# A gated recurrent layer on one core: the order of work before the first step

## The chip, the cores and the metric

The kernel runs on one core of a Trainium2 chip. The metric is the device time of one execution in microseconds (us). The kernel before took 1697.89 us, the median of three runs (1697.15 to 1697.95).

## What is computed

The input x holds 8 sequences of 512 time steps with 512 features. A recurrent layer with a state of 512 values for each sequence runs over the steps and its states are added to x:

```python
def step(h, x_t):
    fused = sigmoid(concatenate([x_t, h], axis=-1) @ w_W + w_b)
    hidden_state, output_state = split(fused, 2, axis=-1)
    memory_state = x_t @ wx_W + wx_b + hidden_state * (h @ wh_W + wh_b)
    h_new = output_state * h + (1.0 - output_state) * tanh(memory_state)
    return (h_new, h_new)
_, hs = scan(step, h0, swapaxes(x, 0, 1))
return x + swapaxes(hs, 0, 1)
```

All numbers are float32. A step needs the state of the step before it, so the 512 steps follow each other; the products of x don't need the state and can be made ahead.

## The kernel before

The state lies transposed: units on the 128 partitions, in four blocks `k` = 0 to 3 of 128 units, the 8 sequences in the free dimension. Blocks 0 and 1 are half A, blocks 2 and 3 half B, with tiles of their own (`hTA`, `hTB`). Four steps make a group (`GS = 4`, so 32 columns of state or of x: 4 steps x 8 sequences), and 16 steps make a chunk of x (`TC = 16`, tiles `xin`, 32 chunks).

A matrix product has a 128x32 block of the state or of x as its stationary operand and a block of weights as the moving one. Its result is 32 rows high, so four products, for `j` = 0 to 3, are put side by side on the four column groups of TensorE and write to the four quarters of the partitions of one PSUM bank. All products go through the helper `mm` (L149). Products accumulate in PSUM, and only one with `start=True` begins anew.

There are eight PSUM banks. Six of 128 columns, `R`, `G` and `H`, in two sets that alternate by group (`banks`), hold the sums from which a step's gates are read. Two of 512 columns (`xps`) hold what x and the biases give for a group: `prefill` (L188) is a generator that makes, for one block `k` at a time, the four products of x with 384 columns of `wx` and yields. `spread` (L200) copies a third of such a bank to `R`, `G` or `H` on ScalarE, `turn_x` (L205) transposes the remaining part into `md1` on VectorE, and `seed` (L184) writes the biases, kept in the tile `bias`, back to the bank with a ScalarE copy, so that it can take the group after next.

Order is that of the program, engine by engine, from `tc.manual_schedule()` (L142) on. Ahead of that line a scheduler may move instructions; the loads and memsets lie there. SyncE (SP) issues all large loads in one queue: x chunk 0 (L87, called at L97), four transfers of `wx` (L101, one for each `k`), six of `wh` (L106: one for each of `k` = 0, 1, 2 and three, R, G and H, for `k` = 3), then the chunks 1 to 3 of x, which the steps 0 to 2 ask for. The state `hin` (L96) and the four bias rows (`rows4`, L94, one partition of each quarter) are asked for on ScalarE's queue.

What PE does before the steps: each of the six banks is zeroed by four products of a zeros tile (L155), both `xps` banks get the biases by products of `ones` and `rows4` with `start=True` (L158), a copy of the second is kept in `bias` (L162), and the two groups' x products follow, alternating by `k` (L218). Then come 16 products of zeros into a bank that doesn't mind them (`warm`, L169, four in each call, called four times at L222). `spread`, `turn_x` and `seed` for group 0 follow.

Step 0 has an order of its own, `FIRST` (L28), in which each "-" is a call of `warm`; `R0` is the four products of bank R with block 0 of the state. Each `k` needs its own transfer of `wh`. All other steps use `ORDER` (L26). Behind the products of each step one piece of `prefill` for the group after next is taken (L249), in step 0 that is block 0 of group 2, which is steps 8 to 11.

The rest of a step: VectorE transposes R, ScalarE makes the sigmoid, and so on over `turn_h`, `turn_z`, `memory` and `update` to the new state, half A before half B. GpSimd adds the state to x (L351) for the output tile `ot`, which SP stores for each chunk.

## Time and profile before

| | us |
|---|---|
| median of 3 runs | 1697.89 |
| the profiled execution | 1697.85 |
| its span, from first to last instruction | 1696.1 |
| PE busy (share) | 1683.8 (99%) |
| VectorE, ScalarE, GpSimd busy | 1087.7, 922.8, 230.1 |
| first product of PE | 1.59 |
| x products done, zero products of L222 begin | 16.82 |
| first product with the state (step 0) | 17.69 |
| first product of step 1, of step 2 | 24.32, 27.69 |
| last product ends, last store is issued | about 1692, 1693.69 |

The span is counted from the first instruction, and all times below are us from there. "PE" in a profile is the matmul side of TensorE, "PEld" its loading of weights. All matmuls stand under L150, the body of `mm`, so they are told apart by their tiles: `R<-zeros` is a zeroing product, `xp<-rows,ones` a bias product, `xp<-wx,xin` an x product and `R<-wh,hTA` one with the state. A float32 matmul appears as two records, so four products are "x8".

### The profile page before, as it was taken

The numbers are of one execution on the slowest core, as the hardware profiler recorded it, in microseconds if no ns is written. First come the engines' busy times: TensorE is split into PE (matmuls) and PEld (weight loads), VectorE is DVE, ScalarE is ACT, GpSimd is POOL, SyncE is SP. The second block draws the span as 40 slices with busy tenths as digits, with TensorE's granted clock in tenths as the row PEclk, the third lists the DMA queues.
The fourth block names the chain that finished last, engine by engine and source line by source line (L and its number), as shares of the span: only waits on it lengthen the run. The fifth ranks groups of instructions, "written<-read, shape, count | busy, mean of one in ns | idle before, by whom it ended". The sixth has DMA issues, their size and how long they took to land.

```text
span 1696.1 us, 121805 instructions
## 1 busy us (share of the span) xinstructions
PE 1683.8 (99%) x53440; PEld 1467.6 (87%) x53440; DVE 1087.7 (64%) x8229; ACT 922.8 (54%) x5121; POOL 230.1 (14%) x1031
## 2 busy tenths in 40 slices
PE   8999999999999999999999999999999999999998
PEld 6888888888888888888888888888888888888887
DVE  4666666666666666666666666666666666666666
ACT  3555555555555555555555555555555555555554
POOL 0111111111111111111111111111111111111111
PEclk9999999999999999999999999999999999999999
DMA  4000000000000000000000000000000000000000
GB/s 177 17 4 17 17 17 17 17 5 17 17 17 17 5 17 17 17 17 5 17 18 17 17 15 6 17 17 17 17 4 17 17 17 17 5 17 11 11 11 10
DMA packets 11485, 30.88 MB, mean 18 GB/s; under 512 B 1348, under 2 KB 1604, under 8 KB 10952
## 3 DMA queue, kind: packets, MB, share of 16 engines
q1 hardware_dynamic: 10800, 23.07, 4.0%
q8 instruction: 417, 6.83, 1.6%
q14 instruction: 116, 0.95, 0.2%
q10 hardware_dynamic: 152, 0.02, 0.0%
HBM read 14.70 MB, written 8.39 MB: 14 GB/s over the span
## 4 chain that ended last, share of the span: by engine, by line
PE 99%; DVE 1%; DMA 0%; ACT 0%; issue 0%; ACTq 0%; DVEq 0%
PE R L150 26%; PE G L150 26%; PE H L150 26%; PE xp L150 20%; DMA rows<-in_bias_dram 0%; DVE md1A L290 0%; DVE hTA L256 0%; ACT hd0A L178 0%; ACT hTA L178 0%; DVE tz L272 0%; DVE bias L162 0%; ACTq L94 0%; DVE rows L92 0%; DVE tr L272 0%; ACT hTB L178 0%
## 5 line engine op out<-in xcount | busy, mean ns | idle before, releaser
L150 PEld LDWEIGHTS R<-wh,hTA 128*32 128x32 f32 x8192 | 243.3, 135 | 212.2 <-DVE hTA L256 212.2
L150 PE MATMUL xp<-wx,xin 128*32 128x384 f32 x4096 | 426.7, 486 | 0.2 <-DVE bias L162 0.2
L272 DVE STREAM_TRANSPOSE tr<-R 128x64 f32<-128x64 f32 x1024 | 194.9, 229 | 313.4 <-PE R L150 313.4
L351 POOL TENSOR_TENSOR ot<-xin,hTB 128x16 f32<-128x16 f32 x511 | 127.6, 250 | 1458.6 <-DVE hTB L256 1366.8
L150 PE MATMUL R<-wh,hTA 128*32 128x128 f32 x8192 | 321.4, 273 | 2.8 <-DVE hTA L256 2.8
L150 PE MATMUL H<-wh,hTB 128*32 128x128 f32 x8192 | 321.3, 273 | 0.0
L150 PE MATMUL R<-wh,hTB 128*32 128x128 f32 x8192 | 321.1, 273 | 0.0
L150 PE MATMUL G<-wh,hTB 128*32 128x128 f32 x8192 | 321.0, 273 | 0.0
L150 PE MATMUL H<-wh,hTA 128*32 128x128 f32 x8192 | 321.0, 273 | 0.0
L150 PE MATMUL G<-wh,hTA 128*32 128x128 f32 x8192 | 321.0, 273 | 0.0
L178 ACT ACTIVATE hd0B<-tz 128x16 f32<-128x16 f32 x512 | 114.8, 224 | 304.9 <-DVE tz L272 304.9
L178 ACT ACTIVATE md0A<-tr 128x16 f32<-128x16 f32 x512 | 120.6, 236 | 256.8 <-DVE tr L272 256.8
L150 PEld LDWEIGHTS G<-wh,hTA 128*32 128x32 f32 x8192 | 250.2, 136 | 0.0
L150 PEld LDWEIGHTS H<-wh,hTA 128*32 128x32 f32 x8192 | 249.8, 136 | 0.0
L150 PEld LDWEIGHTS H<-wh,hTB 128*32 128x32 f32 x8192 | 244.1, 122 | 0.1
L150 PEld LDWEIGHTS G<-wh,hTB 128*32 128x32 f32 x8192 | 243.9, 122 | 0.0
L150 PEld LDWEIGHTS R<-wh,hTB 128*32 128x32 f32 x8192 | 241.2, 122 | 0.1
L256 DVE TENSOR_TENSOR_SCAN hTA<-hd0A,hTA 128x48 f32<-128x48 f32 x512 | 132.0, 258 | 149.2 <-ACT hTA L178 149.2
L256 DVE TENSOR_TENSOR_SCAN hTB<-hd0B,hTB 128x24 f32<-128x24 f32 x1024 | 157.8, 196 | 103.8 <-ACT hTB L178 103.8
L178 ACT ACTIVATE hd0A<-tz 128x16 f32<-128x16 f32 x512 | 118.6, 232 | 111.2 <-DVE tz L272 111.2
L290 DVE STREAM_TRANSPOSE md1A<-G 128x64 f32<-128x64 f32 x512 | 158.9, 310 | 28.7
L178 ACT ACTIVATE hTB<-hTB 128x16 f32<-128x16 f32 x512 | 122.0, 238 | 81.9 <-DVE hTB L256 81.2
(50 smaller groups left out, 1661.9 us busy)
## 6 DMA issues: line engine op xcount, KB each, us to landing
xin<-in_x_dram SPq DMA_DIRECT2D x32, 256.0 KB, 4.0
out_dram<-ot SPq DMA_DIRECT2D x31, 256.0 KB, 2.5
wx<-in_wx_dram SPq DMA_DIRECT2D x4, 768.0 KB, 6.4
wh<-in_wh_dram SPq DMA_DIRECT2D x3, 768.0 KB, 9.6
wh<-in_wh_dram SPq DMA_DIRECT2D x3, 256.0 KB, 12.2
out_dram<-ot SPq DMA_DIRECT2D x1, 192.0 KB
rows<-in_bias_dram ACTq DMA_DIRECT2D x4, 2.0 KB
out_dram<-ot SPq DMA_DIRECT2D x1, 64.0 KB, 1.5
```

The source lines that it names most:

```text
L150: nc.tensor.matmul(out_, lhsT, rhs, start=start, stop=False, skip_group_check=True)
L178: inst = nc.scalar.activation(out_, in_, func, **kw).ins
L256: nc.vector.tensor_tensor_scan(*[t_[:, :, c_].rearrange("p n c s -> p (n c s)") for t_ in (out_, d0, d1)], 0.0, ALU.mult, ALU.add,)
L272: inst = nc.vector.transpose(t_.rearrange("p c n -> p (c n)"), raw[n][hf]).ins
L290: nc.vector.transpose(md1[hf][g % 2][:, :, :, 0].rearrange("p n c -> p c n"), raw["h"][hf])
L351: return engine.tensor_tensor(ot[:, t, 2 * hf : 2 * hf + 2, :].rearrange("p c n -> p n c"), xins[c][:, 2 * hf : 2 * hf + 2, t * B : t * B ...
```

## The change

The two `xps` banks are zeroed by zero products as the six others are, for which the tile of zeros grows to 512 columns. Their biases come by products without `start=True` behind the x products: that of bank 0 behind `k` = 1, that of bank 1 behind `k` = 2. The four calls of `warm` in front of step 0 are gone. `seed(0)` is gone: in step 0, ahead of `R1`, four bias products with `start=True` fill bank 0 again, and `bias` is copied from there by VectorE. `FIRST` has six "-" in place of twelve. The tile of an x chunk has its two halves of 8 steps one after the other, `[P, 2, 4, 64]`, so that chunk 0 can be fetched in two transfers: the first half in front, the second behind all of `wh`; all readers of x use `x_of`. The host lays x out to match. The request for `hin` stands ahead of the bias rows. The first activation, which loads a table, is a sigmoid in place of a tanh.

```diff
-FIRST = "R0 G0 H0 - - - - R1 G1 H1 - - - - R2 G2 H2 - - - - R3 G3 H3"
+FIRST = "R0 G0 H0 - - R1 G1 H1 - - - - R2 G2 H2 R3 G3 H3"
...
-    def load_x(c):
+    def load_x(c, half=slice(0, 2)):
+
         if c < NCH:
-            t_ = xin_p.tile([P, NQ, TC * B], F32, tag="xin", name=f"xin_{c}")
-            nc.sync.dma_start(out=t_, in_=x[c].rearrange("p (k n) -> p k n", k=NQ))
-            xins[c] = t_
+            if c not in xins:
+                xins[c] = xin_p.tile([P, 2, NQ, TC * B // 2], F32, tag="xin", name=f"xin_{c}")
+            nc.sync.dma_start(
+                out=xins[c][:, half], in_=x[c].rearrange("p (e k n) -> p e k n", e=2, k=NQ)[:, half]
+            )
+
+    def x_of(c, k, t, n):
+
+        e, t = divmod(t, TC // 2)
+        return xins[c][:, e, k, t * B : (t + n) * B]
+
+    hin = const.tile([P, NQ, B], F32, name="hin")
+    nc.scalar.dma_start(out=hin, in_=h0)
...
-    hin = const.tile([P, NQ, B], F32, name="hin")
-    nc.scalar.dma_start(out=hin, in_=h0)
-    load_x(0)
+    load_x(0, 0)
...
+    load_x(0, 1)
...
-    zeros = const.tile([P, 128], F32, name="zeros")
+    zeros = const.tile([P, 512], F32, name="zeros")
...
-    nc.scalar.activation(const.tile([P, 1], F32, name="table"), zeros[:, :1], AF.Tanh)
+    nc.scalar.activation(const.tile([P, 1], F32, name="table"), zeros[:, :1], AF.Sigmoid)
...
-    for t_ in list(banks[0].values()) + list(banks[1].values()):
+    for t_ in list(banks[0].values()) + list(banks[1].values()) + xps:
         for j in range(NQ):
-            mm(t_[32 * j : 32 * j + 32, :], zeros[:, :32], zeros, start=True)
-    for t_ in xps:
-        for j in range(NQ):
-            mm(t_[32 * j : 32 * j + 32, :], ones[:, j], rows4, start=True)
-    bias = const.tile([P, 512], F32, name="bias")
-    nc.vector.tensor_copy(bias, xps[1])
+            mm(t_[32 * j : 32 * j + 32, :], zeros[:, :32], zeros[:, : t_.shape[1]], start=True)
...
+    def bias_of(q, start=False):
+
+        for j in range(NQ):
+            mm(xps[q][32 * j : 32 * j + 32, :], ones[:, j], rows4, start)
+
     def warm():
         for j in range(NQ):
-            mm(banks[1]["H"][32 * j : 32 * j + 32, :], zeros[:, :32], zeros)
+            mm(banks[1]["H"][32 * j : 32 * j + 32, :], zeros[:, :32], zeros[:, :128])
...
     for k in range(NQ):
         for it in both:
             take(it, 1)
-    for _ in range(4):
-        warm()
+        if k > 0 and k < 3:
+            bias_of(k - 1)
     spread(0, "RGH")
     for e in range(NQ):
         turn_x(0, e)
-    seed(0)
+    bias = const.tile([P, 512], F32, name="bias")
...
+            if n == "R1" and i == 0:
+                bias_of(0, start=True)
+                nc.vector.tensor_copy(bias, xps[0])
```

In `prefill` and in the adds of GpSimd the slices of `xins[c]` are replaced by `x_of(...)` with the same elements.

More of the change, by code (lines that the diff above doesn't have):

```diff
@@ L194, in prefill @@
                     xps[g % 2][32 * j : 32 * j + 32, 64:448],
-                    xins[c][:, k, t0 * B : t0 * B + 32],
+                    x_of(c, k, t0, GS),
                     wx[:, k, j, :],
@@ L328, in tile_cond_rnn_residual @@
                 ot[:, t, :2, :].rearrange("p c n -> p n c"),
-                xins[c][:, :2, t * B : t * B + B].rearrange("p c n -> p n c"),
+                x_of(c, slice(0, 2), t, 1).rearrange("p c n -> p n c"),
                 state(0, T),
@@ L352, in add @@
                 ot[:, t, 2 * hf : 2 * hf + 2, :].rearrange("p c n -> p n c"),
-                xins[c][:, 2 * hf : 2 * hf + 2, t * B : t * B + B].rearrange("p c n -> p n c"),
+                x_of(c, slice(2 * hf, 2 * hf + 2), t, 1).rearrange("p c n -> p n c"),
                 state(hf, i + 1),
@@ L420 @@
     xd = units(_np.moveaxis(x, 2, 0))
-    xd = xd.reshape(128, 4, Bn, NCH, TC).transpose(3, 0, 1, 4, 2)
+    xd = xd.reshape(128, 4, Bn, NCH, 2, TC // 2).transpose(3, 0, 4, 1, 5, 2)
     xd = c_(xd).reshape(NCH, 128, 4 * TC * Bn)
```

## The prediction

> **What bounds the kernel now.** I read the page first: TensorE (PE) is busy for 99% of the span, its granted clock is near full, and VectorE, ScalarE and the DMA engines have room. Then the chain of waits, in order of time:

> ```profile
> 2.50 5.42 DMA rows<-in_bias_dram
> 7.92 0.14 issue
> 8.05 3.46 PE xp L150 x16
> ...
> 11.53 0.70 DVE bias L162
> 12.23 0.04 issue
> 12.28 4.72 PE xp L150 x56
> ...
> 24.01 0.27 DVE hTA L256
> 24.28 0.04 issue
> 24.32 0.32 PE R L150
> ```

> See that the start hangs on the bias rows (landed at 7.92), on 16 records of bias products, on x products, and at 24.32 on the first new state, where step 1 begins. From there PE works without a break. Between 24.32 and 1690 the waits of PE alone add up to this:

> ```profile
> PE R L150 <- DVE hTA L256: 2.8, 8, 0.4
> ```

> So 511 steps take about (1692 - 24.32)/511 = 3.26 us each, PE-bound, and what the change can move is the instant at which step 1 starts. The timeline of PE up to there:

> ```profile
> 8.05 3.41 PE L150 MATMUL xp<-rows,ones 128*32 128x512 f32 x16 [3.67 <-DMA rows<-in_bias_dram]
> 11.28 0.83 PE L150 MATMUL xp<-wx,xin 128*32 128x384 f32 x8
> 12.28 4.72 PE L150 MATMUL xp<-wx,xin 128*32 128x384 f32 x56 [0.17 <-DVE bias L162]
> 16.82 1.06 PE L150 MATMUL H<-zeros 128*32 128x128 f32 x32
> 17.69 0.40 PE L150 MATMUL R<-wh,hTA 128*32 128x128 f32 x8
> ...
> 22.49 0.40 PE L150 MATMUL G<-wh,hTB 128*32 128x128 f32 x8
> 22.71 0.59 PE L150 MATMUL H<-wh,hTB 128*32 128x128 f32 x7
> ```

> One matmul is two records, and four matmuls on the four column groups (a "quad" below) run side by side. Prices of a quad from start to start: 128 columns 0.43 us cold (R at 1.59, G at 2.02) and 0.22 warm (17.69, 17.91); 384 columns 0.65 warm (seven quads, 12.28 to 16.82); 512 columns 1.7 cold (two in 3.41), and by columns 0.65 x 512/384 = 0.86 warm. That cold and warm exist is seen in the windows (last columns: granted clock, DMA share, GB/s):

> ```profile
> 4.28:7.69 3.41, 0.10 (x4) 0.00 (x0) 2.15 (x11) 0.02 (x1) 0.00 (x0) 1.00 1.01 391
> 7.69:11.10 3.41, 3.05 (x16) 0.90 (x20) 0.00 (x0) 0.00 (x0) 0.00 (x0) 0.50 1.03 429
> 11.10:14.50 3.40, 3.23 (x40) 1.07 (x36) 1.01 (x5) 0.00 (x0) 0.00 (x0) 1.00 1.01 403
> 14.50:17.90 3.40, 3.40 (x72) 1.99 (x68) 0.51 (x4) 0.84 (x4) 0.00 (x0) 1.00 1.01 404
> 17.90:21.30 3.40, 3.40 (x134) 3.40 (x129) 0.00 (x0) 1.62 (x2) 0.00 (x0) 1.00 0.82 314
> ```

> PE idle for one stretch of 3.41 us, then half clock for the next. (Before 4.28 the records hold no clock; the 0.43 quads show that it was cold.) And the DMA share is 1.0 until about 20: the loads of weights are the second limit, now hidden. From the DMA section of each issue (KB, us from issue to landing):

> ```profile
> wh<-in_wh_dram SPq DMA_DIRECT2D x2, 256.0 KB, 12.2
> xin<-in_x_dram SPq DMA_DIRECT2D x1, 256.0 KB, 11.2
> ```

> The last wh transfer, issued at 8.43, lands at 20.6; the next x chunk, issued at 10.02, at 21.2. The trace's completion records give the others: wx 6.05, 8.17, 10.01, 11.86; wh 13.74, 15.70, then 18.71, 19.34, 19.97, 20.61. The jump of 3.0 us before 18.71 is one engine: the other fifteen finish that transfer by 17.55. At 15.94 a 16 KB instruction transfer of 0.97 us sits on the same DMA engines (the DMA view from 15.9 on shows it as queue q8), and the laggard stays about 1.1 us behind to the end.

> [...] the trace has 3% (fell) and 79% (2.69 of 3.41 from 0.87, rose). [...]

> **The change part by part.** Origin as in the profile before. Less x in front: the first transfer shrinks from 256 to 128 KB; the queue moves about 0.41 MB per us, so all of wx and wh land 0.3 us sooner. From landing to PE I take 0.13 (7.92 to 8.05).

> *In front.* The zeros tile is four times as wide: its memset costs 485 ns (rows, 128x512) instead of 165, so PE starts at 1.59 + 0.32 = 1.91. Six 128-wide quads, 6 x 0.43, to 4.47; then two 512-wide, warm 1.72 or cold 3.4, to 6.2 or 7.9. No wait for the bias rows. The h0 request was already ahead of the rows on ScalarE's queue in the trace (0.74), so that edit is worth 0.

> *x products.* Chunk 0 (two quads, 1.3): 6.2 to 7.5, wx landed at 5.75. Chunk 1: wx at 7.87, 8.0 to 9.3. Bias of bank 0, 0.86 warm instead of 1.7 cold, to 10.2 (rows in at 7.9). Chunk 2 to 11.5, bias of bank 1 to 12.3, chunk 3 to 13.6. Before: 16.82. That is 3.2 us won, and the 16 zero products behind it (four quads, 0.87) go too. The copies to R, G, H follow bank 0 by 0.25 to 0.84 us (16.42 to 17.01 before) and lie beside bank 1's last quad.

> *Step 0.* It had 12 zero quads; 6 remain, and the new bias quad (0.86) equals 4: net 0.43 less. R0 G0 H0 0.65 to 14.3, two zero quads to 14.7, the bias quad (waits for VectorE's four transposes, done by about 14.4) to 15.6. Its copy to SBUF, 0.69 on VectorE, has nothing behind it before the R transposes; ScalarE loses the copy of 0.59 and the second table load of 1.28, both of which lay in its idle time: 0. wh of k = 1 at 15.4: 15.6 to 16.2; four zero quads to 17.1. If the instruction transfer, which now comes earlier since PE consumes sooner, slows an engine there, up to 1.2 later; this is still hidden, for now the loads bind: k = 2 at 18.71 - 0.3 + 0.13 = 18.5, done 19.2; R3 19.2; G3 at 19.97 - 0.17 = 19.8; H3 at 20.44 to 20.66.

> *The end of step 0.* Before, step 1 started 24.32 - 22.49 = 1.83 after G3, over transposes, sigmoid, scan, tanh and update. So the state is there at 19.8 + 1.83 = 21.6. The x product of group 2 now reads the second half of x, queued behind all wh on SP. SP issues it once the third wx has landed (9.7)[...]; half of the 0.62 between the last wh and x1 gives 20.6, PE at 20.75, done at 21.4. Also its wait for the bias copy (done by about 16.5) is void. The x chunks 1 to 3 are asked for one issue later (0.33 each); nobody reads them before group 4. On GpSimd's first add the added wait (x half) is met long before.

> Step 1 starts at max(21.4, 21.6) = 21.6 instead of 24.32: 2.7 us. H3's half of the state is behind A's update on VectorE in both, so nothing is lost there. The remaining steps have the same instructions; the x layout only changes strides (GpSimd adds, 250 ns two times a step, idle else). The profiled execution took 1697.85 us for a span of 1696.1; 1697.85 - 2.7 = 1695.15. The median of before, 1697.89, lies 0.04 above it, so I forecast 1695.1.

> **Unknown costs.** Clock at the start: if the rise at 4.28 is missed, the x side ends at about 14.8 to 15.2 instead of 13.6; R3 would be ready at about 17.7 + 1.6 and the wh wait of 19.2 covers it, so 0 to 0.1. The collision with the instruction transfer: from 0 (everything after lands 1.1 sooner) to a second one on the same engine (another 1.1 later). A clock drop in step 0: 0 to 1.7 per half-clock window of dense work.

> **The rivals.**
> *B, no laggard.* The transfer of instructions falls earlier and costs the last wh nothing. G3's weights then land at 18.85 - 0.3, G3 runs at 18.7, step 1 starts at 20.5: 3.8 us, 1694.0. For it: only one engine of sixteen lagged, and why it lost 1.1 to 1.5 us to a 0.97 us transfer is not shown. Against: the queue is full, so a lag once caught has no time to vanish.
> *C, the second half of x comes late.* A second instruction transfer (20.63 before, about 18.5 now) hits the lagging engine[...]: x at 21.7, x product done at 22.5 and the step likewise 0.9 to 1.4 later: 1696.3. Against: before, successive ones did not show on one engine.
> *D, the clock falls in step 0.* The zero products before R3 are gone and PE waits for wh: from 17.0 to 20.4 it may be busy for only 1.1 of 3.41 us, 32%. If that counts as idle, the next window of dense work runs at half clock: 1.7 lost, 1696.8.
> *E, slower than before.* The same drop, but PE does not recover in one window: each dense half-clock window costs 1.71 us, so from 2.7/1.71 = 1.6 windows on the change loses. Two give 1695.1 + 3.4 = 1698.5; slower by over 0.2% needs 3.6 windows. Against: from 21.6 on PE is fully busy, and before, one such window (7.69 to 11.10) was enough.

> **How the numbers follow.** Forecast 42% (own range 1694.4 to 1695.8), B 37%, C 8%, D 9%, E 4%. B is high because the lag rests on one instance. The range 1693.6 to 1696.9 takes in B, C and D. 0.2% (3.4 us) is about what a measurement of this kernel can tell from no change; the bound is 1694.5. Faster by more: nine tenths of B (34) and a quarter of the forecast's cases (11), 45%. Slower by more than 3.4 us: 2%. The rest, 53%, within.

> **What would show it.** Right: the zero quads end by 6 to 8; the last x product before 15.3; PE idle only in step 0, ended by DMA of wh; R<-wh,hTA of step 1 at about 21.6; later steps unchanged. B: that start at about 20.5. C: PE waiting for xin at the end of step 0. D, E: granted clock 0.5 after 18. Wrong altogether if steps behind step 1 differ by more than 5 ns each (2.7/511).

## The result and the profile after

| | before | after |
|---|---|---|
| median of 22 runs, us | 1698.36 (1697.15 to 1698.88) | 1695.11 (1694.78 to 1695.78) |
| profiled execution | 1697.85 | 1695.25 |
| its span | 1696.1 | 1693.5 |
| x products done | 16.82 | 14.33 (13.03 + 2 x 0.65) |
| first product of step 1 | 24.32 | 21.46 |

The ratio is 0.9982, with a 95% interval from 0.9976 to 0.9989: 3.25 us less by the medians, 2.6 by the two profiled executions. The three runs of before that the prediction knew had 1697.89 as their median, the 22 have 1698.36; that is half a microsecond of the difference.

The timeline of PE in the changed kernel, from the zeroing of the x banks on (start, duration, what, and in brackets the idle time ahead of it and what ended it):

```profile
4.55 3.07 PE L159 MATMUL xp<-zeros 128*32 128x512 f32 x16
7.45 2.75 PE L159 MATMUL xp<-wx,xin 128*32 128x384 f32 x32
10.03 1.03 PE L159 MATMUL xp<-rows,ones 128*32 128x512 f32 x8
...
13.03 1.46 PE L159 MATMUL xp<-wx,xin 128*32 128x384 f32 x16
14.73 0.45 PE L159 MATMUL R<-wh,hTA 128*32 128x128 f32 x8 [0.24 <-DMA wh<-in_wh_dram]
...
19.72 0.44 PE L159 MATMUL G<-wh,hTB 128*32 128x128 f32 x8 [0.30 <-DMA wh<-in_wh_dram]
20.36 0.44 PE L159 MATMUL H<-wh,hTB 128*32 128x128 f32 x8 [0.20 <-DMA wh<-in_wh_dram]
20.77 0.85 PE L159 MATMUL xp<-wx,xin 128*32 128x384 f32 x8
21.46 0.67 PE L159 MATMUL R<-wh,hTA 128*32 128x128 f32 x16
```

Three new waits, all ended by a transfer of wh, none of which was there before. The bias rows end no wait any more: their products stand at 10.03, where the rows have long landed, and a quad (four products side by side) of 512 columns takes 0.86 there (10.03 to 10.88), not 1.7. The chain of waits says the same in another way:

```profile
1.64 6.15 DMA wx<-in_wx_dram
7.79 0.02 issue
7.81 0.33 SPq L114
8.14 0.04 issue
8.18 12.13 DMA wh<-in_wh_dram
20.32 0.04 issue
20.36 0.44 PE H L159 x8
20.80 0.83 PE xp L159 x8
```

Up to 20.32 the path is loads, where before it was bias rows, x products and zero products. It is followed by the last wh (H of k = 3), the x product and step 1. The windows, to be held against those before (busy time of PE, PEld, VectorE, ScalarE, GpSimd, then granted clock, DMA share and GB/s):

```profile
4.28:7.69 3.41, 3.41 (x32) 1.07 (x28) 2.81 (x17) 0.02 (x1) 0.00 (x0) 1.00 1.01 413
7.69:11.10 3.41, 3.41 (x44) 1.20 (x40) 0.00 (x0) 0.00 (x0) 0.00 (x0) 1.00 1.02 427
```

PE is busy throughout where it stood idle (4.28 to 7.69), and the window after it has the full clock instead of half. The 1.00 of the first of these windows holds from 6.91 on alone: the clock record begins there, and up to then the zero products of 512 columns went at about the half clock's pace (2.90 for two quads, 4.55 to 7.45, where two of 0.86 would be 1.72). The steps themselves are as they were: measured at the update of half A, a step takes 3.264 us before and 3.265 after in the median, and from the first to the last update it is 1668.15 before and 1668.24 after.

### The profile page after: what moved, and what is told of

Its sections match the earlier page's. It is cut to its first block, busy times and chain, and to the rows that moved or that the text cites. A ratio compares the mean times of both kernels' runs of the same rounds, so it can differ in the third digit from the quotient of the medians.

```text
span 1693.5 us, 121691 instructions
## 1 busy us (share of the span) xinstructions
PE 1684.1 (99%) x53384; PEld 1466.7 (87%) x53384; DVE 1088.0 (64%) x8229; ACT 921.2 (54%) x5119; POOL 229.2 (14%) x1031
## 4 chain that ended last, share of the span: by engine, by line
PE 98%; DMA 1%; DVE 0%; ACT 0%; issue 0%; SPq 0%
PE R L159 26%; PE G L159 26%; PE H L159 26%; PE xp L159 19%; DMA wh<-in_wh_dram 1%; DMA wx<-in_wx_dram 0%; DVE md1A L302 0%; DVE hTA L268 0%; ACT hd0A L187 0%; ACT hTA L187 0%; DVE tz L284 0%; SPq L109 0%; SPq L89 0%; SPq L114 0%; ACT hTB L187 0%
## 5 line engine op out<-in xcount | busy, mean ns | idle before, releaser
L159 PE MATMUL xp<-wx,xin 128*32 128x384 f32 x4096 | 433.7, 486 | 0.0
L159 PE MATMUL R<-wh,hTA 128*32 128x128 f32 x8192 | 328.6, 273 | 2.8 <-DVE hTA L268 2.5
L159 PE MATMUL G<-wh,hTB 128*32 128x128 f32 x8192 | 328.1, 273 | 0.3 <-DMA wh<-in_wh_dram 0.3
L159 PE MATMUL H<-wh,hTB 128*32 128x128 f32 x8192 | 328.0, 273 | 0.2 <-DMA wh<-in_wh_dram 0.2
L159 PE MATMUL R<-wh,hTB 128*32 128x128 f32 x8192 | 328.1, 273 | 0.0
L159 PE MATMUL G<-wh,hTA 128*32 128x128 f32 x8192 | 328.1, 273 | 0.0
L159 PE MATMUL H<-wh,hTA 128*32 128x128 f32 x8192 | 328.1, 273 | 0.0
L159 PEld LDWEIGHTS H<-wh,hTA 128*32 128x32 f32 x8192 | 259.4, 137 | 0.0
L159 PEld LDWEIGHTS G<-wh,hTA 128*32 128x32 f32 x8192 | 259.3, 137 | 0.0
L159 PEld LDWEIGHTS G<-wh,hTB 128*32 128x32 f32 x8192 | 250.4, 122 | 0.6 <-DMA wh<-in_wh_dram 0.6
## 6 DMA issues: line engine op xcount, KB each, us to landing
xin<-in_x_dram SPq DMA_DIRECT2D x31, 256.0 KB, 3.2
out_dram<-ot SPq DMA_DIRECT2D x31, 256.0 KB, 2.4
wh<-in_wh_dram SPq DMA_DIRECT2D x3, 256.0 KB, 11.9
```

What stands on the lines that cost most here:

```text
L159: nc.tensor.matmul(out_, lhsT, rhs, start=start, stop=False, skip_group_check=True)
```

## The experiments

Twelve runs follow, each measured beside the kernel before on the same chip. Since that neighbour moved between 1697.76 and 1698.36 from one set of runs to the next, each is given with its own.

| run | edit | median | its before | step 1 starts (profile) |
|---|---|---|---|---|
| e1 | before, fewer zero products | 1695.58 | 1698.02 | 22.35 |
| e2 | after, all zero products back | 1697.26 | 1698.02 | 23.80 |
| e3 | after, x chunk 0 in one transfer | 1695.16 | 1698.02 | 21.41 |
| e4 | after, no zero product in step 0 | 1695.00 | 1698.02 | 21.32 |
| e5 | before, PE kept busy until the rows land | 1696.73 | 1697.76 | 22.40 |
| e6 | after, banks zeroed by 128-row products | 1695.31 | 1697.76 | 21.44 |
| e7 | after, x products in the waits | 1695.11 | 1697.76 | 21.59 |
| e8 | after again | 1694.92 | 1697.83 | 20.98 |
| e9 | e2, quads as 128-row products | 1697.68 | 1697.83 | 23.35 |
| e10 | before, quads as 128-row products | 1699.56 | 1697.83 | 26.55 |
| e11 | e7, other order | 1695.58 | 1697.83 | 21.30 |
| e12 | e2, four quads as one of 512 columns | 1696.18 | 1698.25 | 23.08 |

**e1: the zero products alone.**

```diff
-FIRST = "R0 G0 H0 - - - - R1 G1 H1 - - - - R2 G2 H2 - - - - R3 G3 H3"
+FIRST = "R0 G0 H0 - - R1 G1 H1 - - - - R2 G2 H2 R3 G3 H3"
...
-    for _ in range(4):
-        warm()
```

> The kernel before with one part of the change alone: the four warm calls in front of step 0 are gone and FIRST is the new one (six zero quads instead of twelve). Theory (loads of wh bind as soon as PE's own order is shorter): x side ends at 16.8 as before, R3 at about 20.1, G3 at 20.3, H3 just behind the last wh (20.7), step 1 starts at about 22.2 instead of 24.3; about 2.2 us less than before (1696.2 of 1698.4). Rival 1 (the zero products are needed for the clock): half clock after 18, gain under 0.5 us or a loss. Rival 2 (PE's time simply adds up and no load binds): ten quads of 0.22, R3 waits for nothing, PE shows no DMA wait.

Measured: 2.44 less than its neighbour, ratio 0.9985 (0.9979 to 0.9992), and step 1 at 22.35. The waits of PE from 4 to 26 us (time waited for, number, longest):

```profile
PE xp L150 <- DMA rows<-in_bias_dram: 3.6, 1, 3.6
PE R L150 <- DVE hTA L254: 0.6, 1, 0.6
```

No load of wh ends a wait, since PE's own order reaches R3 only at 20.30 and H3 at 20.74, and the last wh landed at 20.09 here. So Rival 2 is what happened, and the theory that the loads bind already here is not. Rival 1 did not happen: the clock, which rose only at 12.38 in this execution, stayed full from there. Taking out ten quads brings most of the gain by itself.

**e2: the x side alone**, the changed kernel with the old `FIRST` and the four `warm` calls.

> The changed kernel with all zero products put back (four warm calls in front of step 0, twelve in it); only the x side, the bias order and the x halves are changed. Theory: x side ends at 14.3, PE's own order reaches R3 at 20.6 and H3 at 21.1, step 1 at about 22.6, so +1.2 us against the changed kernel (1696.3), and about 2.1 less than before. With e1 (2.2 less) the two parts then sum to over 4 us while together they bring 3.3: the loads cap them. Rival (the zero products cost nothing, they lie in load waits): 1695.1. Rival (parts add up): +2.2, 1697.3.

Measured: only 0.76 below its neighbour, ratio 0.9997 (0.9989 to 1.0006), a microsecond worse than expected. The number is that of the rival "parts add up", but the timeline of PE shows another reason, a wait that nobody had foreseen:

```profile
19.47 1.07 PE L159 MATMUL H<-zeros 128*32 128x128 f32 x29
21.56 0.30 PE L159 MATMUL H<-zeros 128*32 128x128 f32 x2 [1.03 <-issue]
...
23.80 0.67 PE L159 MATMUL R<-wh,hTA 128*32 128x128 f32 x16 [0.53 <-DVE hTA L270]
```

In the middle of a row of zero products, which wait for nothing, PE stood still for 1.03 us, and what ended it is "issue": nothing the profile shows. A 16 KB instruction transfer began at 19.10 here and was on the DMA engines until 20.08, among the weights.

**e3: one transfer of x in front.**

```diff
-    load_x(0, 0)
+    load_x(0)
...
-    load_x(0, 1)
```

> The changed kernel with chunk 0 of x in one transfer of 256 KB in front. Theory (loads bind at the end of step 0): every wh lands 0.3 us later and step 1 starts 0.3 later, 1695.4. Rival (PE's order binds, or the laggard decides by its own time): 1695.1, no difference. Rival (the second half of x queued behind wh had cost time): below 1695.1.

Measured: 1695.16, against 1695.00 of e4 in the same set. G3 ran at 19.66 and H3 at 20.30, no later than in the changed kernel (19.72 and 20.36), but a single pair can't decide it, since H3 ran at 19.87 when the changed kernel was profiled again (e8). The completion records of the profiles with this order of loads say more: with 256 KB of x in front (before, e1, e3, e5, e10) the last wh landed between 20.09 and 20.61, with 128 KB (after, e2, e4, e6, e8, e9, e12) between 19.83 and 20.66, with means of 20.4 and 20.2. A full 0.3 us is not what they show. By the medians e3 is 2.86 below its neighbour and the changed kernel 3.25 and 2.91 below its own, so what the two transfers of x are worth is not resolved here.

**e4: no zero product in step 0** (`FIRST` without any "-").

> The changed kernel without any zero product in step 0. Theory: PE reaches the wh of k = 1, 2, 3 earlier and waits for them; G3 and H3 start where they did (19.7, 20.4) and step 1 at 21.5: 1695.1 within 0.2. Rival D (waits let the clock fall): granted clock 0.5 for 3.4 us after about 18 to 21, step 1 or 2 at half speed, +1.7: 1696.8.

Measured: 1695.00, as the theory had it. The loads take over all of the time saved (time waited for, number, longest):

```profile
PE R L159 <- DMA wh<-in_wh_dram: 1.9, 2, 1.0
PE H L159 <- DMA wh<-in_wh_dram: 0.2, 1, 0.2
PE xp L159 <- DMA wx<-in_wx_dram: 0.2, 1, 0.2
PE G L159 <- DMA wh<-in_wh_dram: 0.2, 1, 0.2
```

The clock record has one change, up at 4.62, and none of the 19 runs lies above 1695.59, where a half-clock window of dense work would have put 1696.7 (an estimate: 1.7 more, half of the 3.41 us that such a window lasted in before). The idlest window of 3.41 us had PE busy for 2.47; so a share as low as the 32% of rival D did not come up.

**e5: the clock at the bias products.** Thirteen zero quads more behind the zeroing of the banks:

```diff
+    for _ in range(13):
+        for j in range(NQ):
+            mm(banks[1]["H"][32 * j : 32 * j + 32, :], zeros[:, :32], zeros)
```

> The kernel before with 13 more zero quads behind the zeroing of the six banks, so that PE doesn't stand idle until the bias rows land (8.05). Theory (the bias products and the first x product are dear because the clock has fallen during that idle time): bias quads at 0.86 instead of 1.7, x side ends at about 15.1 instead of 16.8, no half-clock window between 7.7 and 11.1, step 1 about 1.7 earlier, 1696.7, and the times of single runs spread less than before's 1.7 us. Rival (the wait for the rows itself is the cost, not the clock): no difference, or 0.3 us slower.

Measured: 1.03 less, ratio 0.9994 (0.9985 to 1.0002), so by the interval of the whole runs the gain is not settled; the trace shows the mechanism:

```profile
7.63 1.92 PE L150 MATMUL xp<-rows,ones 128*32 128x512 f32 x16
9.34 0.86 PE L150 MATMUL xp<-wx,xin 128*32 128x384 f32 x8
10.36 4.72 PE L150 MATMUL xp<-wx,xin 128*32 128x384 f32 x56 [0.16 <-DVE bias L165]
...
23.22 0.33 PE L150 MATMUL R<-wh,hTA 128*32 128x128 f32 x2 [0.17 <-issue]
```

The bias products take 1.92 instead of 3.41 and the x side ends at 14.89, 1.93 earlier, with more work in front than before. Of that, 0.42 is that the rows landed earlier in this execution (the bias products start at 7.63 and not at 8.05); the other 1.51 is the clock, which rose at 5.23 and stayed up. Step 1 starts at 22.40; from there 0.5 us goes lost again, in step 1, at another wait for "issue" (this step takes 3.77 where others take 3.265). The runs lie between 1696.49 and 1697.29, 0.8 apart. That before's wider spread comes from the instant at which the clock rises fits this and was not shown run by run, but three profiles with before's front show the effect: the clock rose for good at 11.11, 12.38 and 13.31 (before, e1, e10), and the x side ended at 16.82, 17.03 and about 17.55.

**e6: where the laggard comes from.**

```diff
-        for j in range(NQ):
-            mm(t_[32 * j : 32 * j + 32, :], zeros[:, :32], zeros[:, : t_.shape[1]], start=True)
+        mm(t_, zeros[:, :128], zeros[:, : t_.shape[1]], start=True)
```

> The changed kernel with each of the eight banks zeroed by one product of 128 rows in place of four of 32: 24 matmuls, 96 TensorE instructions, fewer in front. Theory (the laggard DMA engine comes from the 16 KB instruction transfer that TensorE's progress asks for): that transfer moves from 11.8 to about 15, the first wh lands at about 13.4 instead of 14.6, its fifteen engines and the last one close together, while the last wh are still 1.1 to 1.4 late; the time stays at 1695.1 within 0.2. Rival (the laggard has another cause, at a fixed time or place): the first wh again at 14.6 with one engine 1.3 behind.

Measured: 1695.31, and the instruction transfer moved from 11.84 to 14.95. The first wh was asked for at 5.66 in both. The DMA view of that stretch, for the changed kernel and then for e6 (the last number is the time from issue to landing, known for the first of the two):

```profile
wh<-in_wh_dram SPq DMA_DIRECT2D x2, 768.0 KB, 8.9
```

```profile
wh<-in_wh_dram SPq DMA_DIRECT2D x2, 768.0 KB, 7.7
```

It lands at 14.6 with the transfer in its way and at 13.4 without. In the completion records of the changed kernel, fifteen engines are done by 13.24 and the sixteenth by 14.60; in e6 the last two are 0.13 apart (13.26 and 13.39). The last wh lands late in both, by the same records: in the changed kernel 1.4 behind the fifteenth engine (20.32 against 18.93), in e6 1.2 (20.29 against 19.09), where the instruction transfer only came at 14.95. In these two profiles one engine falls behind when that transfer joins the loads, and is still 1.2 to 1.4 behind at the last wh.

The other profiles agree. Where the first instruction transfer began between 11.35 and 12.40 (nine of them), the first wh has its last engine 0.8 to 1.4 behind the fifteenth. Where it began between 14.95 and 16.20 (before, e1, e6, e10), that is 0.3 at most, and the third wh has 1.1 to 1.3. In e5 it began at 9.49, and the last wx already has 1.2.

**e7 and e11: versions meant to beat both.** In e7 all zero products of step 0 give way to the x products of group 2, with the second half of x and R, G of k = 2, 3 loaded earlier:

```diff
-FIRST = "R0 G0 H0 - - R1 G1 H1 - - - - R2 G2 H2 R3 G3 H3"
+FIRST = "R0 G0 H0 R1 G1 H1 X X R2 G2 R3 G3 X H2 H3 X"
...
```

"X" takes one piece of `prefill`. e11 has `"R0 G0 H0 R1 G1 H1 R2 G2 R3 G3 X X H2 H3"` and leaves the other two pieces to steps 1 and 2.

> A version meant to beat both: no zero products in step 0; in their place, in the waits for wh, all four x products of group 2 (two ahead of R2, one ahead of H2, one behind H3); for this the second half of x is asked for ahead of the wh of k = 2 and 3, and R and G of k = 2, 3 ahead of H. Theory: step 1 starts at about 21.5 as now, and steps 1 to 3, freed of one x product (0.65) each, are then bound by the chain over the new state (about 3.0 instead of 3.27): 0.7 less, 1694.4. Rival (the chain, not PE, sets those steps already): 1695.1. Rival (0.3 us later wh eats it): 1695.4.

> A second try at a version that beats both: as e7, but in step 0 R and G of all blocks go first, two x products of group 2 fill the wait for H of k = 2 and 3, and the other two follow in steps 1 and 2. Theory (e7 showed that the chain over the new state, not PE, sets a step without an x product): the chain of half A starts 1 us earlier (G3 at about 18.4), step 1 at about 20.5, but half B still waits for the last H, so the gain is 0.5 to 0.6: 1694.5. Rival (half B sets all): 1695.0.

Measured: 1695.11 and 1695.58; neither beats the changed kernel (1694.92 beside e11), and both forecasts missed; the rival of e7 (the chain over the state sets those steps) had its 1695.1. The starts of steps 1 to 4 in e7:

```profile
21.59 0.62 PE L159 MATMUL R<-wh,hTA 128*32 128x128 f32 x16
24.76 0.67 PE L159 MATMUL R<-wh,hTA 128*32 128x128 f32 x16 [0.36 <-DVE hTA L271]
28.04 0.67 PE L159 MATMUL R<-wh,hTA 128*32 128x128 f32 x16 [0.37 <-DVE hTA L271]
31.25 0.67 PE L159 MATMUL R<-wh,hTA 128*32 128x128 f32 x16 [0.36 <-DVE hTA L271]
```

A step freed of 0.65 us of PE work takes 3.17 to 3.28 us, hardly less than 3.265: PE waits 0.36 for the state instead. The x products lie in the shadow of the chain over the state, so moving them ahead is worth almost nothing; my estimate of 3.0 for that chain was wrong. In e11 half A was ready earlier, but R2 waited 0.29 for half B and that step took 3.81.

**e8: the changed kernel again.**

> The changed kernel itself once more, as the neighbour for the three others, since the kernel before moved between 1697.8 and 1698.4 from one set of runs to the next: 1695.1, step 1 at 21.5.

Measured: 1694.92, ratio 0.9983 (0.9977 to 0.9990). Step 1 started at 20.98, half a microsecond sooner than expected, since the last wh landed at 19.83 here.

**e9, e10, e12: does e2 run out of instructions?** In e9 and e10 a quad of zero products is one product with 128 rows; the cut is from e9, which also has the `FIRST` and the `warm` calls of e2:

```diff
-        for j in range(NQ):
-            mm(banks[1]["H"][32 * j : 32 * j + 32, :], zeros[:, :32], zeros[:, :128])
+        mm(banks[1]["H"], zeros[:, :128], zeros[:, :128])
```

In e12 four quads are one of 512 columns into the second x bank, one in front of step 0 and three in it:

```diff
-FIRST = "R0 G0 H0 - - R1 G1 H1 - - - - R2 G2 H2 R3 G3 H3"
+FIRST = "R0 G0 H0 - R1 G1 H1 - R2 G2 H2 - R3 G3 H3"
...
-            mm(banks[1]["H"][32 * j : 32 * j + 32, :], zeros[:, :32], zeros[:, :128])
+            mm(xps[1][32 * j : 32 * j + 32, :], zeros[:, :32], zeros)
...
+    warm()
```

> As e2 (the changed kernel with all zero products put back), but each quad of zero products is one product with 128 rows: the same time on TensorE, a quarter of the instructions (sixteen quads, 192 instructions fewer). Theory (the 1.03 us idle in e2 at 20.5, put down to issue, is TensorE out of instructions because the second instruction transfer waits among the weight loads): no such idle time, R3 at about 20.4, step 1 at about 22.4 instead of 23.8, 1696.0 instead of 1697.3. Rival (it is the zero products' own cost or a load): the idle time stays, 1697.3.

> The kernel before with each quad of its zero products behind the x side and in step 0 as one product of 128 rows. Theory (the profiled execution of before shows no idle time for instructions, and what its runs spread over, 1696.9 to 1698.9, comes from the clock's window): no change of the median beyond 0.3, the same spread. Rival (part of before's time, in the runs that are not profiled, is instruction starvation): 0.5 or more below before, and less spread.

> As e2 (all zero products back), but each four quads of 128 columns are one quad of 512 columns into the second x bank: the same time on TensorE (0.86 instead of 0.87) and a quarter of the instructions, without the change of tile shape that made e9 and e10 dear (1.09 for four, and some 0.2 between the shapes). Theory (the 1.03 us idle in e2 is TensorE out of instructions): no idle time, R3 at about 20.4, step 1 at about 22.4 where e2 had 23.8, about 1 us below e2: 1696.1. Rival (the idle time has to do with the zero products or the loads at that place): step 1 at 23.8 again, 1697.3.

e9 lost the idle time but not the microsecond: the replacement is dearer, as the timeline of e9 shows.

```profile
17.95 0.40 PE L159 MATMUL H<-wh,hTA 128*32 128x128 f32 x8
18.28 1.16 PE L159 MATMUL H<-zeros 128*128 128x128 f32 x8
19.37 0.44 PE L159 MATMUL R<-wh,hTB 128*32 128x128 f32 x8
```

From H1 to R2 are 1.42 us; H1 takes 0.22 of it, so four such products cost 1.2 with the change of shape there and back, where four quads cost 0.87. That is 0.33 more, once ahead of step 0 and three times in it. e10 pays it too, which is about 1.3 of the 1.73 by which it lies above its neighbour. Its forecast of no change failed on that price, and what it was meant to tell of before's spread stays open. e12 has the same PE time as e2 and a quarter of those instructions:

```profile
20.18 1.03 PE L159 MATMUL xp<-zeros 128*32 128x512 f32 x8
21.04 0.39 PE L159 MATMUL R<-wh,hTB 128*32 128x128 f32 x8
...
23.08 0.67 PE L159 MATMUL R<-wh,hTA 128*32 128x128 f32 x16 [0.57 <-DVE hTA L269]
```

No idle time at that place, 1696.18: 2.07 below its neighbour where e2 was 0.76 below. R3 came at 21.04 and step 1 at 23.08, both later than expected, because in this profile the clock rose only at 7.82 and the x side ended at 14.78 (13.85 in e2). So the idle time of e2 (1.03) goes with the number of instructions, and not with the time of the zero products on PE; that PE had run out of instructions there is inferred from this.

The other profiles agree. In before, e2, e3 and e8 PE pauses behind the same number of TensorE records (698 or 699 weight loads and products), whatever comes next: H3 of step 0, a zero product, or products of step 1. The pause ends 1.3 to 1.5 us after the second instruction transfer has (in e2 at 21.56 after 20.08, in e8 at 22.37 after 21.04). In e5 it comes behind 954 records, 1.36 after the end of the third. The line at which it shows in e3, with the one behind it:

```profile
22.34 0.87 PE L158 MATMUL R<-wh,hTB 128*32 128x128 f32 x15
22.90 0.37 PE L158 MATMUL G<-wh,hTB 128*32 128x128 f32 x3
```

The sixteenth product record of R comes only after three of G, at 23.05. Step 1 takes 3.55 there, and 3.45 in e8, which is the changed kernel itself, instead of 3.265.

## Why the prediction was right

*The new bound.* "Step 1 starts at max(21.4, 21.6)": measured 21.46. The x product was done at 21.45 and the state came at 21.41, so the two limits were within 0.05 of each other, as the sum had them within 0.2. G3 at 19.72 (19.8), H3 at 20.36 (20.44). Waits of PE only in step 0, ended by wh, as named. e4 shows it from the other side: six quads fewer, 1.3 us of PE, change nothing.

*Parts do not add.* The zero products alone bring 2.4 (e1), the x side alone 2.1 (e12, without the pause of e2), together 2.9 to 3.3. Neither e1 nor e12 shows a wait for wh. In the profile of the changed kernel PE's own order would have reached G3 at 18.68 (14.33, 16 quads of 0.22 and the bias quad of 0.86), and it ran at 19.72: 1.04 of the missing 1.2 to 1.6 is waiting for wh there. In e8 it is only 0.5, so the share differs from one execution to the next.

*The x side.* Predicted end 13.6, measured 14.33, since the clock rose at 6.91 in this execution and not at 4.28; the prediction had 14.8 to 15.2 as the bad case. That this is hidden behind wh is seen in e4 and e6: there the clock rose at 4.62 and 4.82, the x side ended at 13.57 and 13.48, and step 1 still started at 21.32 and 21.44. That the half clock made the bias products dear is shown by e5 (1.92 for the four quads at full clock, 3.41 at 0.50 in before).

*The laggard.* The forecast (lag stays) held against B, and e6 shows its cause: at the first wh the last engine is 0.13 behind the fifteenth without the instruction transfer, and 1.36 with it in the changed kernel. It came earlier now, so wh of k = 1 landed at 16.43 and not at the 15.4 of the sum, which the prediction had among its unknowns and which stayed hidden. B had 37%, which was too much: the argument against it in the prediction (a full queue lets no lag vanish) was the better one here, with 1.36 at 14.60 and still 1.39 at 20.32.

*C, D and E* did not happen. The second half of x landed at 20.64 (the sum had 20.6, C had 21.7), and the x product started at 20.77 (20.75); that is 0.2 us later than PE could have gone on behind H3, a pause which the timeline does not mark. The clock was at 1.0 from 6.91 on, and in e4 from 4.62 on. But the idleness that D asked about never came: between 17.0 and 20.4 PE was busy for 2.91 of 3.41 us, not 1.1. What the clock does at 32% is not tested here.

*Mis-sized: "all of wx and wh land 0.3 us sooner".* In the two profiles they did (20.32 after 20.61), but over the twelve profiles named under e3 the means differ by 0.2, with 0.5 and 0.8 between the earliest and the latest of each kind. The 0.3 is not confirmed, and it didn't show in the sum, because landing times differ by more than that from one execution to the next: in e8 H3 ran at 19.87 and step 1 started at 20.98. (The last wh of before was issued at 8.38, not at 8.43; nothing rests on it.)

*Missed: instructions.* The prediction used the instruction transfer only as a burden on the weights. That PE itself can pause behind it (e2, 1.03 us; e5, 0.5) was no rival. In the profile of the change the second transfer ended at 20.91 and PE came to the record in question only at 22.77, so nothing was lost; in e8, where step 1 started earlier, it cost 0.2. By the distance to the neighbours, the ten more zero quads cost 2.15 to 2.5 us on top of the change (e2); the same PE time with a quarter of the instructions costs 0.8 to 1.2 (e12). So with the faster x side the zero products cost through their instructions too, and taking them out protects what the x side gains.

*The size.* 1695.1 was forecast and 1695.11 measured, but the gain forecast was 2.7 and the medians give 3.25. The profiled executions give 2.60: the start of step 1 moved by 2.86, and 0.26 of it is given back between there and the end, 0.09 in the steps (step 314 alone took 3.37) and 0.17 behind the last update (4.08 instead of 3.91), which was not looked into. The rest is the median of before, which three runs had put half a microsecond too low; the hit to a hundredth is partly luck.

What stays open: how much of before's spread is the clock's rise and how much instructions, and whether an order of loads exists that keeps the instruction transfer off the last weights.

## What to carry to other kernels

When a start-up phase has two limits close together, work out both in time of arrival before pricing any edit: here each part alone brought most of the gain (2.4 and 2.1), and both together 2.9 to 3.3, capped by the loads. Filler work is not free even where PE would have waited: here ten zero quads cost 2.15 to 2.5 us, and 0.8 to 1.2 in a quarter of the instructions, and the 16 KB instruction transfers lay on the same DMA engines as the weights (6.1% of their time from 19 to 20 in e2, beside 98.0% of loads). And filling a wait with work taken from later pays only if the later stage is really bound by that engine: look for what waits there first (in e7 a step without its 0.65 of x products still took 3.17 to 3.28, since PE waited for the state).
